# The second plain feed-forward with unpacking: one list of steps sorted by times in place of three interleaved lists

## The chip, the core and the metric

The kernel runs on one core of a Trainium2 chip. A core has engines that work side by side, each through its own queue, in order: TensorE (PE; its weight loads are PEld) for matrix products and transposes, VectorE (DVE), ScalarE (ACT) and GpSimd (POOL) for work element by element, and SyncE (SP), which here only issues transfers. Semaphores order one engine after another. The metric is the device time of one execution in microseconds (us); lower is better.

## The reference, cut to what matters

The network takes `x`, 2 x 1024 tokens of 256 channels, through eight blocks, each `x = x + f(norm(x))`:

```python
x = x + L0_attn_a(layernorm(x)); x = x + L0_ffn(layernorm(x))
x = x + L0_attn_b(layernorm(x)); x = x + L0_ffn(layernorm(x))     # this one
x = x + L1_attn_a(layernorm(x)); x = x + L1_ffn(layernorm(x))
x = x + L1_attn_b(layernorm(x)); x = x + L1_ffn(layernorm(x))
```

The plain feed-forward `L0_ffn` has three layers of widths 256, 512, 512, 256:

```python
x = relu(x @ W1.T + b1); x = relu(x @ W2.T + b2); out = x @ W3.T + b3
```

`L1_ffn` has its three weight matrices (gate, up, down, 2048 x 256 each) packed as four-bit codes, two to an integer, with one scale to 32 values. A code's low three bits `m` give a magnitude (0, 0.5, 1, 1.5, 2, 3, 4, 6), its fourth bit a sign. The kernel unpacks them once:

```python
a = max(m - 4, 0) + relu(2 * m - 12) + m      # twice the magnitude
w = 0.5 * a * sign * scale
```

## The kernel before

The kernel runs in stages: first attention with most of the first feed-forward, second attention, then the stage of this change (`ffn0_dequantize`): the second plain feed-forward with the unpacking of the later weights beside it. Third attention and the fourth follow, each with an `L1_ffn` that reads the unpacked weights.

Inside such a stage (`in_order`) nothing reorders the work: each engine executes its instructions in the order in which the Python steps are called. So a list of steps, called one after another, is the schedule of all engines at once; only SP's transfers run ahead of it as far as their buffers allow.

**Tokens.** The 2048 tokens are four groups of 512. `ffn0_pieces` gives a group's 22 steps, in this order:

- six for the normalization, in two halves p of 256 tokens: `stats` (`bn_stats`, L242 and L243, on VectorE; the mean is negated on GpSimd, L245), `rows` (the reciprocal root in nine small VectorE operations, L223 to L233; then on GpSimd the normalized rows `ln_xn`, L254, and the bias `x+b3`, L467) and `turn` (four TensorE transposes, L475, and ScalarE's eviction `fxT`, L481). The list holds them as stats 0, rows 0, stats 1, turn 0, rows 1, turn 1;
- four of layer one (`hidden`; one step is two products of 512 columns, L493, then ScalarE's eviction `h` with bias and relu, L500);
- eight of layer two (two steps to an `h`);
- four of layer three (`output`: four products, L509, then VectorE's sum into `x`, L514).

**Weights.** `dequantize` makes 24 parts of 256 columns, each of four steps:

- `codes`: nine transfers on SP, one of codes `pk` (L1434, six buffers) and eight of scales `sc` (L1436, eight buffers);
- `magnitudes`: five VectorE operations (masks `m` and `sg`, L1447 and L1448, and `a = max(m-4, 0)`, L1451), two on ScalarE (`c`, L1452; `sign`, L1453), and `a+c` on GpSimd (L1454);
- `signs`: `a+m` on VectorE (L1458), then `a*sign` on GpSimd (L1459);
- `values`: the write of the weights on VectorE (L1462).

**The order before.** A group's 16 product steps have the next group's `stats` and `rows` woven into layer one and the first half of layer two, and the next group's two `turn` steps into layer three (after its first and its third output). The parts' steps are lagged (`values` of one part, `signs` of the next, `magnitudes` of the one after, `codes` four parts ahead of its `magnitudes`) and then woven evenly, by count, into the whole list of 88 token steps, norms counted like products.

Of the kernel before, what the change touches and what calls it, by code (L numbers as in the profile page):

```python
# [27 lines left out]
def interleave(a, b):  # L28

    ia = ib = 0  # L30
    while ia < len(a) or ib < len(b):
        if ib >= len(b) or (ia < len(a) and ia * len(b) <= ib * len(a)):
            a[ia]()
            ia += 1
        else:
            b[ib]()
            ib += 1


def interleave_into(out, a, b):  # L40

    interleave([lambda x=x: out.append(x) for x in a], [lambda x=x: out.append(x) for x in b])
# [45 lines left out]
        ),  # L88
    ),
    "end": (2.3, 3, 4, 5),  # L90
}


class Net:
# [600 lines left out]
    def ffn0_dequantize(self, ffn, deq):  # L695

        nc, tc = self.nc, self.tc
        with ExitStack() as ctx:
            work = ctx.enter_context(tc.tile_pool(name="f_work", bufs=2))
            ps = ctx.enter_context(tc.tile_pool(name="f_ps", bufs=1, space=PSUM))  # L700

            def bank(name):
                return ps.tile([P, 512], F32, tag="g", name=name, bufs=8)

            ctx.enter_context(self.in_order())
            products = []
            after = [
                [step for _, step in self.ffn0_pieces(work, bank, 4 * n, *ffn, scalar=True)]
                for n in range(4)
            ]  # L710


            stats, rows, turned = [
                [after[n][m] for n in range(4) for m in ms] for ms in ((0, 2), (1, 4), (3, 5))
            ]
            products += [stats[0], rows[0], stats[1], rows[1], turned[0], turned[1]]
            for n in range(4):
                norms, turns = [], []
                if n < 3:
                    norms = [stats[2 * n + 2], rows[2 * n + 2], stats[2 * n + 3], rows[2 * n + 3]]  # L720
                    turns = turned[2 * n + 2 : 2 * n + 4]
                interleave_into(products, after[n][6:14], norms)
                products += after[n][14:18]
                interleave_into(products, after[n][18:], turns)
            unpack = []
            for args in deq:
                unpack += self.dequantize(work, *args)


            parts = []  # L730
            for n in range(len(unpack) + 6):
                for m, lag in ((3, 6), (2, 5), (1, 4), (0, 0)):
                    if 0 <= n - lag < len(unpack):
                        parts.append(unpack[n - lag][m])
            interleave(products, parts)

# [1430 lines left out]
```

## Time and profile before

| what | us |
|---|---|
| runs of the kernel: median of 3 (lowest to highest) | 2922.77 (2910.84 to 2925.98) |
| the profiled execution: its own time / its span | 2926.19 / 2924.5 |
| busy in the span: TensorE, VectorE, ScalarE, GpSimd | 2541.0, 1989.2, 1330.9, 1016.8 |
| this stage, first statistics to the end | 894.2 to 1047.0: 152.8 |
| busy in the stage: TensorE, VectorE, ScalarE, GpSimd | 124.9, 118.6, 53.6, 92.1 |

The span runs from the first to the last instruction of one profiled execution; the 1.7 us between it and that execution's own time lie around it. The profile names each instruction by its line, its engine, and what it writes and reads; a bracket shows how long its engine stood idle before it and who released it. An engine counts as busy from an instruction's start to its end, also while the instruction cannot get at its data. In the windows of the profile, busy times are listed for PE, PEld, DVE, ACT and POOL, followed by the granted TensorE clock (1.00 is full speed), the busy share of the transfer engines and GB/s.

### The profile page before, as it was taken

To read this page: it belongs to the slowest core of one execution; us is meant where nothing else is said; L and a number is where in the kernel's file an instruction comes from. 1 tells how busy PE (TensorE), PEld (TensorE's weight loads), DVE (VectorE), ACT (ScalarE), POOL (GpSimd) and SP (SyncE) were. 2 spreads that over 40 slices of the span, in tenths; PEclk is the share of its full clock that TensorE was granted. 3 is DMA by queue.
4 is the path that set the end of the run, shared out by engine and by line. 5 is a ranking of instruction groups with operands and counts; after the bars stand their busy time and mean duration, and the time that the engine had idled before them with its cause. 6 is when DMAs were issued, how large, how long until landed. Compare 5 with 4: busy or idle time off the path is not lost.

```text
span 2924.5 us, 66842 instructions
## 1 busy us (share of the span) xinstructions
PE 2541.0 (87%) x26384; PEld 1575.5 (54%) x26384; DVE 1989.2 (68%) x6786; ACT 1330.9 (46%) x2800; POOL 1016.8 (35%) x1568
## 2 busy tenths in 40 slices
PE   6999998999997877988888888888787888899888
PEld 2334334444433444656555555555565776777777
DVE  5777774766756758679776888787656655665551
ACT  2686860345453345676666666767321211221110
POOL 3444332211115657667555665565300000000000
PEclk9999998899998976999998999998887999998999
DMA  3000000000001100000000000000011010110100
GB/s 120 1 1 1 1 1 0 1 1 1 1 1 47 40 1 1 1 1 1 1 1 1 1 1 1 1 1 1 20 23 25 17 24 17 24 31 17 24 9 15
DMA packets 61978, 35.37 MB, mean 12 GB/s; under 512 B 43216, under 2 KB 58080, under 8 KB 61664
## 3 DMA queue, kind: packets, MB, share of 16 engines
q1 hardware_dynamic: 59472, 29.49, 3.9%
q8 instruction: 207, 3.39, 0.5%
q10 hardware_dynamic: 2192, 1.61, 0.2%
q14 instruction: 107, 0.88, 0.1%
HBM read 22.68 MB, written 8.39 MB: 11 GB/s over the span
## 4 chain that ended last, share of the span: by engine, by line
PE 60%; DVE 20%; POOL 5%; issue 5%; ACT 5%; SPq 1%; DMA 0%; POOLq 0%; ACTq 0%; DVEq 0%
PE ph L1494 5%; PE po L2003 5%; PE pg L1990 5%; PE pu L1990 4%; DVE p L1257 4%; PE ph L493 4%; PE s L871 4%; PE e L1246 3%; PE dT L1318 3%; PE s L906 3%; PE py L925 2%; PE po L1513 2%; PE s L602 2%; DVE p L1296 2%; PE py L627 2%
## 5 line engine op out<-in xcount | busy, mean ns | idle before, releaser
L1267 ACT ACTIVATE p<-p,nm 128x128 f32<-128x128 f32 (+7 forms) x512 | 390.8, 768 | 79.4 <-DVE nm L1263 42.4
L1257 DVE CUSTOM_DVE_ANT_0 p<-e,mask 128x512 f32<-128x512 f32 (+3 forms) x768 | 382.2, 552 | 55.3 <-PE e L1246 54.8
L1304 POOL TENSOR_SCALAR p<-p,md 128x128 f32<-128x128 f32 (+7 forms) x256 | 241.3, 947 | 175.1 <-DVE md L1296 154.3
L1332 ACT ACTIVATE pT<-dT 128x384 f32<-128x384 f32 (+3 forms) x384 | 176.4, 487 | 202.5 <-PE dT L1318 201.5
L245 POOL TENSOR_SCALAR ln_mv<-ln_mv 128x2 f32<-128x2 f32 x64 | 15.7, 246 | 724.6 <-DVE ln_mv L243 722.2
L1246 PE MATMUL e<-kT,qT 32*128 32x512 f32 (+3 forms) x1536 | 228.4, 574 | 44.2 <-DVE nm L1257 41.3
L1318 PE MATMUL dT<-ident,p 128*128 128x128 f32 x1152 | 196.7, 297 | 64.3 <-POOL p L1304 35.7
L1296 DVE CUSTOM_DVE_ANT_0 p<-p,nrs 128x128 f32<-128x128 f32 (+7 forms) x256 | 221.6, 891 | 26.2 <-POOL p L1288 26.0
L911 ACT ACTIVATE pr<-s 128x512 f32<-128x512 f32 (+3 forms) x384 | 157.3, 496 | 165.0 <-PE s L906 156.3
L1284 POOL TENSOR_SCALAR p<-p,ra,neg_lam 128x128 f32<-128x128 f32 (+7 forms) x256 | 219.6, 858 | 9.1
L1318 PEld LDWEIGHTS dT<-ident,p 128*128 128x128 f32 x1152 | 137.3, 148 | 152.7 <-POOL p L1304 66.5
L608 ACT ACTIVATE pr<-s 128x1024 f32<-128x1024 f32 (+1 forms) x192 | 145.4, 813 | 131.9 <-PE s L602 82.8
L1990 PE MATMUL pg<-xT,gate 128*128 128x256 f32 x576 | 152.9, 412 | 7.5 <-ACT xT L274 5.5
L2003 PE MATMUL po<-down,inter 128*128 128x256 f32 x576 | 157.7, 436 | 1.9 <-DVE x L2010 1.2
L871 PE MATMUL s<-kT,qT 32*128 32x512 f32 (+3 forms) x768 | 155.1, 521 | 4.7 <-DVE q_pad L879 2.9
L879 DVE CUSTOM_DVE_ANT_0 masked<-s,mask 128x128 f32<-128x128 f32 (+3 forms) x256 | 110.7, 487 | 61.8 <-PE s L871 61.7
L613 ACT ACTIVATE pr<-pr 128x1024 f32<-128x1024 f32 (+1 forms) x192 | 152.1, 852 | 0.0
L1246 PEld LDWEIGHTS e<-kT,qT 32*128 32x128 f32 x1536 | 84.5, 201 | 116.3 <-DVE nm L1257 73.2
L616 POOL TENSOR_SCALAR_AFFINE_SELECT pr<-pr 128x256 f32<-128x256 f32 x128 | 90.9, 728 | 154.7 <-ACT pr L613 62.5
L1996 DVE TENSOR_TENSOR inter<-inter,pu 128x512 f32<-128x512 f32 x72 | 49.3, 685 | 132.6 <-PE pu L1990 132.6
L2003 PEld LDWEIGHTS po<-down,inter 128*128 128x128 f32 x576 | 124.5, 221 | 24.4 <-DVE x L2010 2.0
L1990 PE MATMUL pu<-xT,up 128*128 128x256 f32 x576 | 137.5, 382 | 0.2 <-DVE inter L1996 0.2
(295 smaller groups left out, 5375.2 us busy)
## 6 DMA issues: line engine op xcount, KB each, us to landing
uk_d<-uk SPq DMA_DIRECT2D x128, 32.0 KB, 1.9
r<-uk_d SPq DMA_DIRECT2D x8, 512.0 KB, 3.2
x<-in_L_attn_a_X SPq DMA_DIRECT2D x4, 512.0 KB, 6.9
qh_d<-qh SPq DMA_DIRECT2D x8, 256.0 KB, 2.8
o<-qh_d SPq DMA_DIRECT2D x128, 16.0 KB, 1.7
out<-x SPq DMA_DIRECT2D x4, 512.0 KB, 3.1
w<-in_L_ffn_W2T SPq DMA_DIRECT2D x1, 1024.0 KB, 8.5
pk<-in_L_ffn_gate_packed SPq DMA_DIRECT2D x8, 128.0 KB, 2.5
```

Of the source, the lines that this page charges most:

```text
L871: nc.tensor.matmul(tiles[g][:, 0:n], shared["qT"][rows, t, j * P : (j + 1) * P], kT[rows, lo : lo + n], start=True, stop=True,)
L911: nc.scalar.activation(pr[:, g, off:512], tiles[g][:, 0:m], AF.Exp, scale=0.25)
L1246: nc.tensor.matmul(own.tiles[h][:, a, 0 : hi - lo], made["q"][r : r + 32, a, t, :], kT[r : r + 32, a, lo:hi], start=True, stop=True,)
L1257: nc.vector.tensor_tensor_reduce(own.p[h][a][:, lo:hi], own.tiles[h][:, a, 0 : hi - lo], neg_row[:, T - nk + lo : T - nk + hi], -1.0, 3e38 ...
L1267: nc.scalar.activation(own.p[h][a], own.p[h][a], AF.Exp, bias=own.nm[:, h, a : a + 1], scale=-1.0, accum_out=own.sm[:, h, a : a + 1],)
L1284: nc.gpsimd.tensor_scalar(p1, p1, own.ra[:, h : h + 1], nlam[:, head : head + 1], ALU.mult, ALU.mult)
L1296: nc.vector.tensor_tensor_reduce(p0, p0, p1, own.nrs[:, h : h + 1], 3e38, ALU.add, ALU.min, own.md[:, h : h + 1],)
L1304: nc.gpsimd.tensor_scalar(p0, p0, -1.0, own.md[:, h : h + 1], ALU.mult, ALU.add)
L1318: nc.tensor.transpose(dT[:, n, :], own.p[h][0][:, kb * P : (kb + 1) * P], self.ident)
L1332: nc.scalar.activation(shared[t, s + h][:, lo:hi, :], own.dT[h, part][:, 0 : hi - lo, :], AF.Exp)
L1990: nc.tensor.matmul(ph[:, j, :], m_[:, kc, m * P : (m + 1) * P], f.xT[:, kc, :], start=(kc == 0), stop=(kc == 1),)
L2003: nc.tensor.matmul(f.po[:, b], inter[m // 2][:, m % 2, b * P : (b + 1) * P], wd[:, m % 2, (m // 2) * C : (m // 2 + 1) * C], start=(m == 0) ...
```

## The change

The two weaving loops and the lagged list go. Every step gets a time, in units of one product step, all go into one list, and the list is sorted by time and called.

```diff
+SECOND = {
+    "norms": (-30, -20.1, -11.8, -12, -6.4, -2.4),
+    "unpack": (-7.9, 2.57, (6.7, 7.6, 10.3, 13.8)),
+}
...
-            products += [stats[0], rows[0], stats[1], rows[1], turned[0], turned[1]]
+            timed = []
             for n in range(4):
-                norms, turns = [], []
...
-                interleave_into(products, after[n][6:14], norms)
-                products += after[n][14:18]
-                interleave_into(products, after[n][18:], turns)
...
-            interleave(products, parts)
+                steps = [s for _, s in self.ffn0_pieces(work, bank, 4 * n, *ffn, scalar=True)]
+                timed += zip([16 * n + m for m in SECOND["norms"] + tuple(range(16))], steps)
+            first, every, ahead = SECOND["unpack"]
+            parts = [part for args in deq for part in self.dequantize(work, *args)]
+            for n, part in enumerate(parts):
+                timed += zip([first + every * n + m for m in ahead], part)
+            timed.sort(key=lambda x: x[0])
+            for _, step in timed:
+                step()
```

Group n's products stand at 16n to 16n+15. Its norm steps stand at 16n plus the six times of `norms`, so its first half is turned after the previous group's product 4 (the first of layer two) and its second half before the last two outputs. Statistics of a group's first half stand 30 products ahead, almost two groups; the first half of group 1 has its statistics and rows ahead of the first product of all. Part n of the weights has `codes` at 2.57n - 1.2, `magnitudes` at 2.57n - 0.3, `signs` at 2.57n + 2.4 and `values` at 2.57n + 5.9. So between two parts the order becomes magnitudes of n+1, signs of n, values of n-1, where it was values of n-1, signs of n, magnitudes of n+1. The last `values` stands at 65, behind the last product, which is 63. No instruction is added or removed.

More of the change, by code (lines that the diff above doesn't have):

```diff
@@ L705, in ffn0_dequantize @@
             ctx.enter_context(self.in_order())
[L706 to L715, printed above, removed]
-            products += [stats[0], rows[0], stats[1], rows[1], turned[0], turned[1]]
-            for n in range(4):
-                norms, turns = [], []
-                if n < 3:
-                    norms = [stats[2 * n + 2], rows[2 * n + 2], stats[2 * n + 3], rows[2 * n + 3]]
-                    turns = turned[2 * n + 2 : 2 * n + 4]
-                interleave_into(products, after[n][6:14], norms)
-                products += after[n][14:18]
-                interleave_into(products, after[n][18:], turns)
[L725 to L734, printed above, removed]
-            interleave(products, parts)
+            timed = []
+            for n in range(4):
+                steps = [s for _, s in self.ffn0_pieces(work, bank, 4 * n, *ffn, scalar=True)]
[7 more added lines that the diff above has]
+                step()
     def attn_b(self, w, wo, cos, sin, ffn):
```

## The prediction

> **What bounds the kernel now.** I read the page first (busy shares, then the chain that ended last), then the windows of the one stage that the change touches, then that stage's timeline engine by engine.
>
> The page says that TensorE leads: 87% busy, 60% of the chain. The diff touches one stage alone, the second plain feed-forward, which runs from the first `bn_stats` at 894.20 us (the last sum of the attention before it starts at 893.87) to the last weight write at 1046.30, so 152.8 us with its end. There I looked at TensorE.
>
> ```profile
> 933.96 1.89 PE L509 MATMUL po<-w,h 128*128 128x256 f32 x8
> 941.16 8.92 PE L493 MATMUL ph<-fxT,w 128*128 128x512 f32 x16 [5.31 <-ACT fxT L481]
> ...
> 978.42 9.06 PE L493 MATMUL ph<-fxT,w 128*128 128x512 f32 x16 [5.31 <-ACT fxT L481]
> ...
> 1015.68 9.20 PE L493 MATMUL ph<-fxT,w 128*128 128x512 f32 x16 [5.30 <-ACT fxT L481]
> ```
>
> This is TensorE's timeline: start, length, then in brackets the idle time and who ended it. Each group of 512 tokens starts late by 5.3 us, because the turned tokens `fxT` of the next group are not there. The groups follow one another at 37.0, 37.3 and 37.3 us, while the last, which waits for nothing, needs 29.8 (1015.68 to 1045.5). This looks like 7.4 us to be had at each of three boundaries. But who makes `fxT` late? ScalarE turns it out only after the unpacking pieces queued ahead of it, and those wait for VectorE. So the next view is the other engines.
>
> ```profile
> 904.20:941.20 37.00, 30.62 (x89) 16.32 (x89) 29.06 (x71) 13.26 (x22) 23.90 (x23) 0.92 0.23 60
> 941.20:978.40 37.20, 30.83 (x88) 16.28 (x88) 30.44 (x73) 13.26 (x22) 23.22 (x23) 0.91 0.19 52
> 978.40:1015.70 37.30, 31.03 (x89) 16.46 (x89) 30.54 (x73) 13.36 (x22) 23.30 (x23) 0.91 0.16 41
> 1015.70:1047.00 31.30, 29.83 (x80) 15.89 (x80) 21.21 (x43) 11.36 (x18) 15.75 (x14) 0.93 0.00 1
> ```
>
> Columns: stretch (cut at each group's first product), length, busy us of PE, PEld, DVE, ACT, POOL, then clock and DMA. In a group of 37.2 us VectorE is busy 30.4 and GpSimd 23.2: together 53.7, so they must overlap by 16. Do they?
>
> ```profile
> 915.37 0.67 DVE L1462 SCALAR_TENSOR_TENSOR gate<-a,sc 128x512 f32<-128x512 f32 x1
> ...
> 935.22 1.71 DVE L1462 SCALAR_TENSOR_TENSOR gate<-a,sc 128x512 f32<-128x512 f32 x1
> ...
> 937.78 1.30 DVE L1447 TENSOR_SCALAR m<-pk 128x256 int32<-128x256 int32 x1
> ```
>
> ```profile
> 935.11 1.27 POOL L1454 TENSOR_TENSOR a<-a,c 128x512 f32<-128x512 f32 x1 [0.83 <-DVE a L1451]
> 937.67 1.26 POOL L1459 TENSOR_TENSOR a<-a,sign 128x512 f32<-128x512 f32 x1 [1.29 <-DVE a L1458]
> ```
>
> The weight write takes 0.67 us at 915.37. At 935.22 GpSimd has begun a `TENSOR_TENSOR` 0.11 us before, and the same write ends at 936.93, 0.55 us after GpSimd's end at 936.38. The mask of 0.28 us that starts at 937.78 inside GpSimd's next one takes 1.30. So **a two-input GpSimd operation and most VectorE operations exclude one another**, and VectorE's "busy" contains the time it is shut out. Where VectorE does stand idle (`a L1458` waits 19.1 us for `POOL a L1454` in this stage), it is GpSimd that is running.
>
> The stage is then bounded by one sum: what excludes one another, in a row. GpSimd's two-input work: `a+c` 31.4, `a*sign` 31.6 and `x+b3` 11.2 us, 74.2. VectorE, from start to start where nothing blocks: a part's four masks and `a` 1.15 (900.89 to 902.04 by its pitch), sum 0.60, write 0.60, so 24 x 2.35 = 56.4; eight nine-step reciprocal roots of 1.66 (895.40 to 897.06), 13.3. Together 74.2 + 69.7 = 143.9 of the stage's 152.8 us. Only 8.9 us are left for idle time and for what may lie beside GpSimd (`bn_stats` 8 x 1.2, the 16 sums into `x` at 0.33: 14.9, part of it hidden already). TensorE needs 4 x 29.9 = 120 and waits on this.
>
> Here a rule of the Trainium skill goes against the trace in part. SBUF — State Buffer, "SBUF: two separate sides", says that VectorE and GpSimd share one port pair, an exclusive lock held for a whole instruction, and that the other fully blocks. For the two-input operations the rows above agree. For GpSimd's one-input `ln_xn` they do not: at 914.30 two of them take 2.09 us (1.10 at 897.32) while five mask operations and a write go on beside them, 0.67 us long. By the rule their 15.0 us would belong in the sum, 158.9, longer than the stage itself; by the trace 143.9. I use the trace's. Either way the rule speaks against this change: no order shortens an exclusive sum.
>
> **The change part by part.**
>
> *Counts.* The same 352 matmul records, 24 parts, 8 norms; nothing is removed. Cost 0.
>
> *Transposes beside the second layer.* Per group, TensorE's four transposes for the first half of the next tokens (0.60) move from between outputs to after the first product of layer two; the second half's to before the last two outputs. They need `xn`, whose rows now stand 12 to 20 products earlier. This removes the 5.31 us waits as such: `fxT` is asked for 12 products (some 20 us) ahead for the first half and two outputs (1.7 each, 3.5 us) ahead for the second. What is late next is the port: ScalarE's evictions still stand behind `c` and `sign` of a part, and those behind VectorE's masks. So TensorE will wait elsewhere, in smaller pieces. Worth 0 by itself; if the port were no bound, worth 3 x 5.31 + 1.08 + 1.09 + 0.94 = 19.0 (the last three are waits for `h` after the first layer).
>
> *Parts spaced 2.57 products apart, 6.2 to each 16.* Before, a part's write, the next's sum and the next's masks stand together, so that VectorE waits for GpSimd's `a+c`; after, the order is masks of n+1, sum of n, write of n-1, and each wait has nearly a whole part (4.9 us) of slack. VectorE's 27.8 us of waits for GpSimd (19.1 + 5.8 + 2.9) go, but turn into blocked time: one part costs 2.35 + 2 x 1.27 = 4.89 on the port in either order. What is truly saved is the time with neither at work: the four gaps of 0.61, 0.61, 0.81 and 0.38 in the last group, where `a+c` waits for `c`, `c` for a hidden eviction and this for TensorE, and some 0.3 at each norm. The 24 parts' DMAs, 9 issues of 0.42 to 0.46 us each (4.2 a part), keep their order on SP and their six and eight buffers; 4.2 is under 4.9, so they stay hidden. If SP were late, one landing (1.8) would show once.
>
> *Norms of the second group's first half put ahead.* VectorE does one more pair of statistics (1.2) before the second half's root; the first product starts at about 905.4 instead of 904.18, and the first masks some 3 us later. TensorE has 20 us of slack in the stage, and the norm is work that the port owes anyway: 0. Its statistics buffers are two, so the third must wait until GpSimd's first `ln_xn` has read (898.4; VectorE arrives at 898.26): 0.2 at most.
>
> *Statistics and sums into `x` elsewhere.* They may run beside GpSimd. No row shows their new places. At best all 14.9 are hidden (a part is already, inside the 8.9 left over), at worst the hidden part comes out again: between 0 and +6. They mostly follow masks or a sum, where GpSimd starts next, so I take the good end, 0.
>
> *The tail.* Part 24's masks come 0.4 us ahead of the `c` (0.72), `sign` (0.5) and `h` (0.59) on which the four last outputs (7.07) wait; then a sum and a write: 10.3 us from its first mask. The port owes only 8.0 in that time (1.15 + two sums 1.2 + three writes 1.8 + three times 1.27). So 2.4 us of it lie idle.
>
> *Sum.* Of the 8.9 us left over, 1.2 at the start (the first statistics) and 2.5 at the end stay: 5.2 are won. Profiled execution 2926.19 - 5.2 = 2921.0. The median of the runs, 2922.77, lies 3.4 under that execution, so the figure to compare is 2922.77 - 5.2 = **2917.6**.
>
> **The rivals.**
>
> *TensorE is the bound and its waits were the cost.* For it: TensorE leads the page and its waits at the boundaries are plain. Against it: the 143.9 us. It saves the 19.0: 2903.8.
>
> *In-order queues lock the engines together: slower.* The transposes now stand inside layer two; where `xn` is late, TensorE stops there with all its products behind it, ScalarE's evictions wait, `c` behind these, `a+c` behind `c`, VectorE behind `a+c`: the port idles. The nearest rows are the first transposes, which waited 4.10 and 2.94 for `ln_xn`; at three boundaries 3 x 7.04 = 21.1, so 2943.9. It decides if `ln_xn` lands later than the product that it now stands behind. Against it: rows are listed 8 products (some 15 us) ahead of their transposes.
>
> *The change only moves waits.* No idle time is won, or the hidden statistics come out: -1 to +6, 2922 to 2929.
>
> **How the numbers follow.** 0.5% is 14.6 us, about what a measurement here can tell from no change: the three runs differ by as much. Forecast (2912 to 2922) 0.5; only moved 0.23; TensorE rival 0.17; locked queues 0.1. The first two lie within 0.5%. The TensorE rival's 19 us would be faster; partial outcomes split both outer cases: faster 0.17, same 0.74, slower 0.09. Range: 2902 takes in the TensorE rival, 2930 the upper end of moved waits.
>
> **What would show it.** Right: first-layer products still start 34 to 37 us apart in the first groups; the 5.3 us waits gone; `a L1458` no longer waits for GpSimd but its mean rises from 0.684 us, as it is now shut out; writes still above 1.2 us. Busy VectorE outside GpSimd's two-input work plus that work is again some 144. Wrong: groups 30 to 32 us apart (TensorE rival), or transposes that wait several us for `ln_xn` (locked queues), or blocked time that shrinks with the new order.

## The result, and the profile after

| | before | changed |
|---|---|---|
| median of 12 runs each, us | 2918.01 | 2908.47 |
| lowest to highest, us | 2910.84 to 2926.59 | 2903.53 to 2912.44 |
| ratio, 95% interval | | 0.9960 (0.9948 to 0.9973) |
| profiled execution: time / span, us | 2926.19 / 2924.5 | 2906.75 / 2905.0 |
| the stage, first statistics to end of last weight write, us | 152.8 | 145.6 |

The change saves 9.5 us, 0.3% to 0.5%. The two profiled executions differ by more, 19.4 us, but 11.0 of that lies before the stage begins (894.2 against 883.2), in code that is the same in both: between 400 us and the stage TensorE was granted a clock of 0.94 in the one and 0.97 in the other. So I compare the stage alone. It became 7.2 us shorter in this pair of traces, 11.0 in a repeat (141.8 us).

TensorE's timeline of the changed kernel, at the three boundaries and at the end (start, length, then idle before and releaser; lines of the changed kernel are 9 or 10 off those of before):

```profile
924.38 7.13 PE L502 MATMUL ph<-fxT,w 128*128 128x512 f32 x16
...
954.19 0.98 PE L484 MATMUL ln_t<-ident,ln_xn 128*128 128x128 f32 x4 [2.01 <-POOL ln_xn L263]
955.00 3.62 PE L518 MATMUL po<-w,h 128*128 128x256 f32 x16
958.93 7.13 PE L502 MATMUL ph<-fxT,w 128*128 128x512 f32 x16 [0.31 <-ACT fxT L490]
...
992.62 7.03 PE L502 MATMUL ph<-fxT,w 128*128 128x512 f32 x16
...
1018.54 8.81 PE L518 MATMUL po<-w,h 128*128 128x256 f32 x26 [3.54 <-ACT h L509]
```

The waits of 5.3 us are gone; the first layers start 31.3, 34.5 and 33.7 us apart (37.0, 37.3, 37.3 before). But a group's work needs about 30, so TensorE still waits, now in small pieces elsewhere (2.01 for the rows of the next tokens, 3.54 at the end). The windows by group show why:

```profile
893.10:924.40 31.30, 31.19 (x89) 16.88 (x89) 28.05 (x67) 13.58 (x22) 21.53 (x22) 0.92 0.22 62
924.40:958.90 34.50, 29.61 (x88) 15.75 (x88) 33.55 (x73) 13.01 (x22) 25.36 (x23) 1.00 0.20 56
958.90:992.60 33.70, 29.59 (x88) 15.87 (x89) 33.09 (x65) 13.25 (x22) 26.28 (x21) 1.00 0.19 51
992.60:1028.90 36.30, 31.15 (x81) 16.96 (x79) 30.61 (x49) 12.15 (x20) 22.53 (x18) 0.91 0.02 5
```

Third busy figure, VectorE: 33.55 of 34.50 us, where it was 30.44 of 37.20. VectorE became busier by 15 us in the stage (118.6 to 134.0) and GpSimd by 9 (92.1 to 101.2) with not one instruction more. The groups of the same stage say what that is (busy us, mean ns of one, then idle before and who ended it). First `a+m` before the change, then the three that share the port in the changed kernel:

```profile
L1458 DVE TENSOR_TENSOR a<-a,m 128x512 f32<-128x512 f32 x24 | 16.4, 684 | 19.1 <-POOL a L1454 19.1
```

```profile
L1449 POOL TENSOR_TENSOR a<-a,sign 128x512 f32<-128x512 f32 x24 | 35.5, 1478 | 4.3 <-DVE a L1448 4.3
L1444 POOL TENSOR_TENSOR a<-a,c 128x512 f32<-128x512 f32 x24 | 35.3, 1469 | 26.9 <-ACT c L1442 22.6 <-DVE rsq_z L238 2.6 <-DVE a L1441 1.7
...
L1448 DVE TENSOR_TENSOR a<-a,m 128x512 f32<-128x512 f32 x24 | 18.8, 783 | 2.5 <-POOL a L1444 2.5
```

`a+m` (now L1448) waits 2.5 us for GpSimd instead of 19.1, but takes 783 ns instead of 684, and GpSimd's two operations average 1.47 and 1.48 us instead of 1.31 and 1.32: the wait for a semaphore became a wait inside the instruction.

### The profile page after: what moved, and what is told of

Read it like the earlier page. It is cut to its first block, busy times and chain, and to the rows that moved or that the text cites. A ratio compares the mean times of both kernels' runs of the same rounds, so it can differ in the third digit from the quotient of the medians.

```text
span 2905.0 us, 66838 instructions
## 1 busy us (share of the span) xinstructions
PE 2530.3 (87%) x26384; PEld 1572.5 (54%) x26384; DVE 2003.4 (69%) x6786; ACT 1329.8 (46%) x2800; POOL 1021.7 (35%) x1568
## 4 chain that ended last, share of the span: by engine, by line
PE 39%; DVE 13%; ACT 4%; POOL 4%; issue 4%; DMA 0%; POOLq 0%; ACTq 0%; DVEq 0%
PE ph L1484 5%; PE po L1993 5%; PE pg L1980 5%; PE pu L1980 4%; DVE p L1247 4%; PE e L1236 4%; PE dT L1308 3%; PE po L1503 2%; DVE p L1286 2%; PE py L1338 1%; POOL p L1294 1%; ACT p L1257 1%; POOL p L1274 1%; PE pq L1663 1%; PE kh L1663 1%
```

## The experiments

Each kernel was timed beside runs of the kernel before on the same chip, and profiled once. Stage lengths are from those single profiles; the two of the changed kernel differ by 3.9 us, so a stage difference under about 4 us is not told apart. "Neither at work" is time in the stage with neither VectorE nor a two-input GpSimd operation busy, worked out from the timelines.

| run | stage, us | neither at work | ratio to before (95%) |
|---|---|---|---|
| before | 152.8 | 7.9 | 1 |
| changed | 145.6 | 7.3 | 0.9960 (0.9948 to 0.9973) |
| changed, again | 141.8 | 3.9 | 0.9968 (0.9958 to 0.9979) |
| token steps alone | 149.1 | 6.2 | 0.9994 (0.9979 to 1.0008) |
| weight parts alone | 143.1 | 6.1 | 0.9966 (0.9954 to 0.9978) |
| old order inside a part's cycle | 149.3 | 8.1 | 0.9983 (0.9975 to 0.9992) |
| parts 2.4 apart | 144.3 | 6.8 | 0.9982 (0.9967 to 0.9997) |
| sign on VectorE | 134.1 | 4.7 | 0.9952 (0.9935 to 0.9969) |
| GpSimd out of the parts | 126.6 | 13.2 | 0.9897 (0.9879 to 0.9915) |

**Which half of the change: the token steps alone.** The new times for norms, transposes and products; the parts lagged and woven by count as before.

```diff
-            for n, part in enumerate(parts):
-                timed += zip([first + every * n + m for m in ahead], part)
             timed.sort(key=lambda x: x[0])
...
+            interleave([step for _, step in timed], parts)
```

> The new times for the token steps alone; the weight parts lagged and woven by count, as before. Port theory (what counts is how VectorE's and GpSimd's exclusive work is packed, which the order of the parts sets): the 5.3 us waits of TensorE at the group boundaries go or move, but the stage stays at 150 to 154 us (152.8 before), ratio to before 0.999 to 1.001. TensorE theory (the early transposes are the gain): the whole gain, stage some 145 to 147 us, ratio about 0.996 to 0.997.

```profile
941.85 7.13 PE L502 MATMUL ph<-fxT,w 128*128 128x512 f32 x16 [1.80 <-ACT fxT L490]
...
969.40 3.98 PE L518 MATMUL po<-w,h 128*128 128x256 f32 x10 [3.31 <-ACT h L509]
...
1003.83 4.11 PE L518 MATMUL po<-w,h 128*128 128x256 f32 x10 [2.07 <-ACT h L509]
```

No gain in time; the stage is 1 us under the 150 to 154 expected. The boundary waits shrank to 1.80, nothing and 0.17, and came back as waits for `h` in the middle of a group: the transposes moved, what TensorE waits for did not. Its waits inside the stage still show VectorE in step with GpSimd:

```profile
DVE a L1447 <- POOL a L1443: 23.5, 13, 3.0
```

(us in total, times, longest.) One thing speaks for caution: weaving by count put parts between the first norms, so the first product began 16.1 us into the stage, not 9.9. Had TensorE been the bound, the stage would still have ended at 16.1 + 4 x 29.9 = 136 and not at 149.

**Which half: the weight parts alone.** The token steps keep the order of before and get as their time the number of products ahead of them; the parts get the new times.

> The new times for the weight parts alone; the token steps in their old order, with the next tokens turned between outputs. Port theory: nearly the whole gain, stage 145 to 148 us, ratio 0.996 to 0.998, although TensorE still waits for fxT at each boundary. TensorE theory: no gain, the waits of some 5 us stay and the ratio is 0.999 to 1.001.

The whole gain: 0.9966 and 143.1 us. The transposes stand between the outputs as before, and yet only one boundary still waits:

```profile
994.32 7.13 PE L502 MATMUL ph<-fxT,w 128*128 128x512 f32 x16 [1.16 <-ACT fxT L490]
```

So the port theory's result held, but not its detail: I had expected the waits for `fxT` to stay. Before the change, ScalarE's queue stood behind the parts' masks at the boundaries, as at the first of them:

```profile
939.38 0.72 ACT L1452 ACTIVATE c<-m,minus 128x512 f32<-128x512 int32 x1 [3.60 <-DVE m L1448]
940.01 0.61 ACT L1453 ACTIVATE sign<-sg 128x512 f32<-128x512 int32 x1
940.53 0.58 ACT L481 ACTIVATE fxT<-ln_t 128x512 f32<-128x512 f32 x1
```

With the parts in the new order these waits nearly vanish by themselves. TensorE's waiting does not: it now waits for `h` between outputs, up to 3.40 and 3.66 us.

**What in the parts: order or spacing.** Two of the four part times move, so that the parts stay 2.57 apart but stand in the order of before.

```diff
-    "unpack": (-7.9, 2.57, (6.7, 7.6, 10.3, 13.8)),
+    "unpack": (-7.9, 2.57, (6.7, 7.6, 10.1, 12.6)),
```

> The changed kernel with two of its four part times moved (10.3 to 10.1, 13.8 to 12.6), so that the parts keep their spacing but stand in the order of before: write of n, sum of n+1, masks of n+2. If the order inside a part's cycle is what the new parts gain (each wait has a whole part of slack): the waits of VectorE for a+c come back (19 us in the stage before, 2.5 after), the stage takes 149 to 153 us in place of 145.6, ratio to before 0.998 to 1.000. If the even spacing over products is the gain: as the changed kernel, 145 to 147 us and 0.996.

Half of the gain goes: 0.9983, 149.3 us; `a+m` waits 14.8 us for GpSimd again. Against the 22 runs of the changed kernel on the same chip this run's 22 have a median 4.3 us higher (2915.58 against 2911.30); resampling both sets gives a ratio of 1.0003 to 1.0026 (95%), so the order counts. The spacing seems to count too: 0.9983 lies under 1 with its whole interval, and the new token steps alone gave nothing. First GpSimd and VectorE in this run, then both in the changed kernel, each in its last group:

```profile
1000.64 1.39 POOL L1449 TENSOR_TENSOR a<-a,sign 128x512 f32<-128x512 f32 x1 [1.30 <-DVE a L1448]
1002.86 1.58 POOL L1444 TENSOR_TENSOR a<-a,c 128x512 f32<-128x512 f32 x1 [0.83 <-DVE a L1441]
1005.32 1.39 POOL L1449 TENSOR_TENSOR a<-a,sign 128x512 f32<-128x512 f32 x1 [0.87 <-DVE a L1448]
1007.54 1.58 POOL L1444 TENSOR_TENSOR a<-a,c 128x512 f32<-128x512 f32 x1 [0.84 <-DVE a L1441]
```

```profile
1002.64 0.68 DVE L1452 SCALAR_TENSOR_TENSOR down<-a,sc 128x512 f32<-128x512 f32 x1
1004.48 0.69 DVE L1448 TENSOR_TENSOR a<-a,m 128x512 f32<-128x512 f32 x1 [1.16 <-POOL a L1444]
```

```profile
1008.48 1.57 POOL L1444 TENSOR_TENSOR a<-a,c 128x512 f32<-128x512 f32 x1 [1.25 <-ACT c L1442]
1010.02 1.71 POOL L1449 TENSOR_TENSOR a<-a,sign 128x512 f32<-128x512 f32 x1
1012.98 1.58 POOL L1444 TENSOR_TENSOR a<-a,c 128x512 f32<-128x512 f32 x1 [1.25 <-ACT c L1442]
```

```profile
1008.25 0.68 DVE L1448 TENSOR_TENSOR a<-a,m 128x512 f32<-128x512 f32 x1
1008.85 1.75 DVE L1452 SCALAR_TENSOR_TENSOR down<-a,sc 128x512 f32<-128x512 f32 x1
1010.53 1.35 DVE L1437 TENSOR_SCALAR m<-pk 128x256 int32<-128x256 int32 x1
1011.80 0.28 DVE L1438 TENSOR_SCALAR m<-pk 128x256 int32<-128x256 int32 x1
```

Old order: a part takes 1007.54 - 1002.86 = 4.68 us. New order: 1012.98 - 1008.48 = 4.50. GpSimd's waits for a semaphore (0.83, 0.87) cost nothing in the old order, since VectorE is at work meanwhile. In both orders its `a+c` starts while a VectorE operation still runs (so it is 1.58 and 1.57 us long, with 0.30 of queueing) and ends 1.12 us after that one (1003.32 to 1004.44, 1008.93 to 1010.05). What differs is who follows. In the old order it is `a+m`, which needs this very result: it starts 0.04 us after GpSimd's end and is done 0.73 us after it (1005.17). In the new order the write of another part is already pending (so 1.75 us long) and is done 0.55 us after GpSimd's end (1010.60). That is the 0.18 us.

Of the changed kernel's 23 steps from one `a+m` to the next, 10 take 4.5 us; of this run's, 9 take about 4.67. But only 12 of the 24 `a+m` of this run are started by GpSimd's end, 8 in the kernel before and 1 in the changed one, so 0.18 us for each explains some 2 us here and less before. In the kernel before, the parts of its last group took 5.42, 4.68 and 5.62 (`a+m` at 1022.18, 1027.60, 1032.28, 1037.90), two of them held up by `c`. What remains of the stage, 152.8 to 149.3, goes with the spacing, but 3.5 us is within what single profiles tell apart.

**Is it the port: a*sign on VectorE.**

```diff
-                nc.gpsimd.tensor_tensor(a, a, t["sign"], ALU.mult)
+                nc.vector.tensor_tensor(a, a, t["sign"], ALU.mult)
```

> The changed kernel with the product a*sign of each part on VectorE in place of GpSimd: 24 operations of 0.60 us more on VectorE, 24 of 1.27 us less on GpSimd. Port theory: the exclusive sum falls by 24 x 0.67 = 16 us, until TensorE (120 us and some 10 at the start) bounds the stage: 132 to 137 us, 8 to 13 us under the changed kernel, ratio to before about 0.992 to 0.994. Theory that VectorE alone is the bound (it is busy 134 of 145.7 us): 14 us more work on it, stage 155 to 160, ratio above 1.000.

```profile
889.90:1024.00 134.10, 119.30 (x352) 64.28 (x352) 127.03 (x313) 53.11 (x88) 67.98 (x67) 0.96 0.18 48
```

VectorE got 24 more operations, and its busy time fell from 134.0 to 127.0: it had been waiting, not working. The stage fell to 134.1 us, as the port theory said; more work on a VectorE that was the bound would have made it longer. The ratio, 0.9952, overlaps with the changed kernel's, so here the stage decides, not the total.

**A version that beats both: GpSimd out of the parts.** `max(m-4,0) + m` is `max(m,4) + m - 4`, so two-input operations of VectorE do it in one less step:

```diff
-                nc.vector.tensor_scalar(a, m, 4.0, 0.0, ALU.subtract, ALU.max)
+                nc.vector.scalar_tensor_tensor(a, m, 4.0, m, ALU.max, ALU.add)
-                nc.gpsimd.tensor_tensor(a, a, c, ALU.add)
...
-                nc.vector.tensor_tensor(a, a, t["m"], ALU.add)
-                nc.gpsimd.tensor_tensor(a, a, t["sign"], ALU.mult)
+                nc.vector.scalar_tensor_tensor(a, a, -4.0, t["c"], ALU.add, ALU.add)
+                nc.vector.tensor_tensor(a, a, t["sign"], ALU.mult)
```

(`c` has three buffers in place of two; what that does alone was not tested.)

> The changed kernel with GpSimd out of the parts: max(m,4)+m in one VectorE operation in place of max(m-4,0), then (a-4)+c in one, then a*sign, then the write; per part 0.81 + 4 x 0.60 = 3.2 us on VectorE, nothing on GpSimd. Port theory: 24 x 3.2 + roots 13.3 + x+b3 11.2 + statistics and sums 14.9 = 116 us, under TensorE's 130 with its start, so TensorE bounds the stage: 130 to 134 us, ratio to before 0.992 to 0.995, a little under the run with the sign alone on VectorE (134.1 us). VectorE-bound theory (20 us more of its own work than in the changed kernel, at its busy 134): over 150 us, ratio about 1.000 or more.

```profile
894.50:925.40 30.90, 30.90 (x88) 16.99 (x89) 25.56 (x74) 13.58 (x22) 10.97 (x14) 0.92 0.28 61
925.40:1009.90 84.50, 84.48 (x257) 46.99 (x256) 76.19 (x198) 39.10 (x64) 13.66 (x15) 1.00 0.19 46
```

TensorE has no gap from 894.5 to 1009.9: 115.38 busy of 115.4 us, the last three groups at the full clock. The stage takes 126.6 us, 26 less than before; the run 2892.33 us against 2920.78, ratio 0.9897. Now TensorE is the bound, and only now would its waits have been worth hunting. My estimate of 130 to 134 (ratio 0.992 to 0.995) was too timid: it priced a group at 29.9 us, as TensorE needed before at granted clocks of 0.91 to 0.93; at 1.00 a group takes 28.4 here.

**The tail: parts 2.4 products apart.**

```diff
-    "unpack": (-7.9, 2.57, (6.7, 7.6, 10.3, 13.8)),
+    "unpack": (-7.9, 2.4, (6.7, 7.6, 10.3, 13.8)),
```

> The changed kernel with parts 2.4 products apart in place of 2.57, so that the last masks stand at 54.9 and not at 58.8, four products earlier. Port theory with a tail that I priced too low: the last four outputs no longer wait (3.54 us) for the eviction behind the last masks, and less of the port lies idle at the end: 2 to 5 us under the changed kernel, ratio to before 0.994 to 0.996. If the tail costs nothing: the same as the changed kernel, 0.996.

```profile
952.89 3.42 PE L518 MATMUL po<-w,h 128*128 128x256 f32 x10 [2.55 <-ACT h L509]
...
991.61 4.15 PE L518 MATMUL po<-w,h 128*128 128x256 f32 x10 [5.89 <-ACT h L509]
...
1020.08 7.07 PE L518 MATMUL po<-w,h 128*128 128x256 f32 x32
```

A miss. The last outputs wait for nothing, as expected, but TensorE waits for `h` earlier (3.28, 2.55, 5.89), and nothing is won: 0.9982, if anything less than the changed kernel's 0.9960 and 0.9968. The tail's idle port time was not to be had in this way.

**The changed kernel again.**

> The changed kernel itself, beside the two others on the same chip: stage 145 to 147 us, ratio to before 0.995 to 0.997.

The ratio, 0.9968, is as before within the intervals; the stage, 141.8 us, is 3 us shorter than expected. Two profiles of one kernel can differ by that much. Two places of this trace, of which more below:

```profile
960.24 0.98 PE L484 MATMUL ln_t<-ident,ln_xn 128*128 128x128 f32 x4 [2.02 <-POOL ln_xn L263]
961.06 5.30 PE L518 MATMUL po<-w,h 128*128 128x256 f32 x16
...
1024.60 5.88 PE L518 MATMUL po<-w,h 128*128 128x256 f32 x26 [2.17 <-ACT h L509]
```

## Why the prediction was right, and where not

*The bound.* Right. The port sum decided that 19 us of plain TensorE waits would not turn into 19 us, and the runs bear it out: the token half, with its late first product, gives nothing, the parts half gives the whole gain, work moved from GpSimd to VectorE gives 11.6 us of stage and, all of it, 19.0 (145.6 to 126.6; from the repeat, 7.7 and 15.2). The TensorE rival falls with the first run, where its boundary waits nearly went and no time was won, and with these moves, which leave TensorE's steps as they are; the parts half alone would not decide, since the waits for `fxT` went there too. The locked-queues rival shows as three small waits of the transposes (2.01, 1.67 and 0.50 us), too small to count.

*The size.* Forecast 5.2 us, measured 9.5 (interval of the ratio: 8 to 15 us). The time itself, 2908.47, lies inside the range but under the forecast's own band, 2912 to 2922, and nearer to the TensorE rival's 2903.8; it is the runs, not this number, that tell the two apart. The mis-sized term is the part's price, "2.35 + 2 x 1.27 = 4.89 on the port in either order". Where nothing else came between, it measured 4.50 in the new order and 4.68 in the old one at the same spacing. Of the 0.39 us up to 4.89, about 0.28 is GpSimd's: an operation of it that queues shuts VectorE out for 1.13 us (median), where one that does not takes 1.27. So the sentence "no order shortens an exclusive sum" is wrong: order sets whether the next user of the port is already waiting, and a handover to a waiting user costs less.

*What was saved.* "What is truly saved is the time with neither at work" failed: that time went from 7.9 to 7.3 us only (3.9 in the repeat). The time with one or the other at work, named as a sign to be "again some 144", fell instead, 144.9 to 138.3 (137.9). Of these 6.6 us, 2.4 are statistics and sums into `x` that now run beside a two-input GpSimd operation: 7.7 us of them (8.1 in the repeat) against 5.3 before. I had put that term at 0. Some 3.2 are handovers, by an estimate from counts in the two traces: 27 of GpSimd's 48 operations for the parts queue (over 1.35 us long) in place of 13, for 0.14 us each, and 1 `a+m` in place of 8 is started by GpSimd's end, for 0.18 each. The last 1.0 is not accounted for. That a saving of this size was forecast is therefore in part luck: the term that it was summed from gave 0.6 us in this trace, and terms that it held at nothing gave the rest.

*The tail.* 10.3 us from the last part's first mask to the end were forecast; it took 13.8 (1015.03 to 1028.85). Most of the missing 3.5 us is TensorE's: its last 13 products (26 records) ran at a granted clock of 0.66 after a wait of 3.54 us, 8.81 us long. In the repeat the wait was 2.17, the clock 1.00, the same products took 5.88 us, and the tail took 10.9.

*The start.* The first product comes 9.9 us into the stage, not 11.2: the norm put ahead cost TensorE nothing.

*The signs.* The 5.3 us waits went, `a+m` rose from 684 to 783 ns, the writes stayed above 1.2 us on average (1.32, though 10 of the 24 took 0.9 or less). The starts 34 to 37 us apart were named too high: they are 31.3 to 34.5, and the first lies where the sign of the TensorE rival was put, 30 to 32. By that sign alone the two could not have been told apart.

*The level.* The forecast of 2917.6 was taken from a median of three, 2922.77; that of twelve is 2918.01. Of the 9.1 us by which 2908.47 lies under it, 4.8 are this and 4.3 the gain.

What stays open: how large the spacing's share and the order's are. By the runs the order's is 0.7 to 7.5 us, and what is left to the spacing 2 to 7.

## What to carry to other kernels

When VectorE and GpSimd both look half idle in turns, add up what cannot run at the same time before believing an engine's wait: a waiting engine may only be the shadow of that sum. Then first try to take two-input work off GpSimd, even if VectorE gets more instructions; ordering the rest so that the next user is already pending was worth far less here (7 to 11 us of stage, against another 15 to 19). And hunt TensorE's gaps only once nothing else bounds the stage, as in the version without GpSimd in the parts.

## What the runs showed of the hardware

VectorE's busy time counts the time in which it is shut out: 15 us more of it with the same instructions and a shorter stage, 7 us less with 24 operations more. Not all of VectorE's work is shut out: `bn_stats` and the sums into `x` take 0.39 to 0.42 us whether a two-input GpSimd operation runs beside them or not. GpSimd's one-input `ln_xn` is not shut out but slowed: two of them take 1.10 us beside statistics (897.32 in the kernel before), 2.09 beside masks and a write (914.30 there), up to 2.46 in the changed kernel.

A wait of a few microseconds can cost TensorE twice, where the granted clock falls after it: 3.54 us of waiting was followed by 8.81 us at 0.66 for products that took 5.88 at 1.00 in the repeat. The length of the wait does not decide this alone: after 2.01 us the next 16 records took 3.62 us at 1.00 in the one trace, after 2.02 us 5.30 at 0.68 in the other. What else decides it is not shown here.
